# Layer 0's preparation: normalisation folded into the weights, inverse deviations as columns and a row through DRAM, three stages of blocks, merged writes

## The chip, the cores and the metric

The kernel runs on one core of one Trainium2 chip. The metric is the device time of one execution in microseconds (us), the median over several runs. The engines are TensorE (PE, with its weight loads as PEld), VectorE (DVE), ScalarE (ACT), GpSimd (POOL) and SyncE (SP), which here only issues transfers (DMA). Each engine works through its own instructions in order and waits on semaphores for the others. A DMA is issued by an engine's queue and carried out by 16 DMA engines that all queues share.

## What is computed

Two attention layers over an image `x` of 2 x 256 x 64 x 64, that is 2 batches of N = 4096 tokens with 256 channels. Only layer 0 is touched by the change; the reference for it, cut to what matters:

```python
xf = x.reshape(B, C_, N).transpose(0, 2, 1)
mu = jnp.mean(xf, axis=-1, keepdims=True)
var = jnp.mean(jnp.square(xf - mu), axis=-1, keepdims=True)
xn = (xf - mu) * jax.lax.rsqrt(var + LN_EPS) * norm_w + norm_b
qkv = jnp.einsum('bnc,oc->bno', xn, qkv_w)
q, k, v = jnp.split(qkv, 3, axis=-1)          # 4 heads of 16
attn = jax.nn.softmax(jnp.einsum('bhnd,bhmd->bhnm', q, k) * SCALE, axis=-1)
d1 = jax.nn.relu(jnp.einsum('oc,bchw->bohw', conv1_w, x) + conv1_b[None, :, None, None])
dyn = jnp.einsum('oc,bchw->bohw', conv2_w, d1) + conv2_b[None, :, None, None]
attn = attn * dyn[:, :, :, None]
out = jnp.einsum('bhnm,bhmd->bhnd', attn, v)
out = jnp.einsum('bnr,cr->bnc', out, out_w)   # back to 256 channels
return jax.nn.sigmoid(gamma[0] * out + x)
```

Layer 1 is a second attention with 4 heads of 64, without normalisation and with a residual; it takes layer 0's result.

## The kernel before

The channels lie on the partitions, in two chunks of 128 (`CC` = 2); the tokens of a batch are cut into 8 blocks of 512 (`NB`), 16 blocks in all. The kernel has three stages. The *preparation* turns each block into layer 0's q, k, v and gate. *Layer 0's attention* goes over 16 blocks of queries with 32 steps of 128 keys each (a loop over `t`), and *layer 1's attention* follows. Layer 0's attention needs the largest score of each query first (`maxima`, L398) and runs that 35 steps ahead (`LEAD0`) of the weights; the maxima of the first 32 steps therefore are taken inside the preparation, two steps in each of its last rounds.

The preparation is the loop at L603, `for n in range(len(blocks) + 3)`. Each round works on up to three blocks at different stages: `new` (block n), `middle` (n - 1) and `old` (n - 2), and the calls in the loop's body set the order on every engine, since the instructions made through `seq` keep the order of the program. Instructions made without it, DMA issues above all, are put into their queue where the scheduler finds room. For one block the steps are:

- `prep_sum` (L272, POOL): the two chunks of x are added into `both`, one block ahead of need; `prep_mean` (L279, PE): a product with a matrix of 1/256 gives the mean in every partition, in PSUM.
- `prep_center` (L284): DVE subtracts the mean (`xc`), ACT squares (`sq`), POOL adds the two chunks (`squares`).
- `prep_var`, `prep_std`, `prep_rstd` (L297 to L310), one round later: the same product for the variance, ACT's root over 128 x 512, and DVE's reciprocal in four pieces of 128 x 128.
- `prep_norm` (L312, POOL): `xc` times the inverse deviation, then times `norm_w` plus `norm_b`, a chunk at a time.
- `prep_product` (L324, PE), two rounds after the first step: q and k in one product with `wqk`. `prep_split` (L327): the result is split into three bf16 parts whose sum has the precision of fp32 (ACT, DVE, ACT, POOL), and SyncE writes them to DRAM, six pieces to `kd0` and six to `qd0` of 64 rows each, from which `load_k` (L342) and `load_q` (L390) fetch them back as 96 rows; three more rows of k are ones, set by POOL.
- `prep_values` and `prep_keep_values` (L348, L360): v by PE, copied by ACT into `vs0`. `prep_gate`, `prep_keep_gate`, `prep_dyn` (L369 to L377): conv1, its relu, and conv2 for four blocks at once.

PSUM has eight banks: four in `psw` for all products of the preparation (tag `bank`), two pairs in `psx` for the maxima. After the loop these pools are closed, the constants of the later stages are loaded, and from L751 the steps of layer 0's attention run; small jobs are hung into that loop by `at(t, place, step)`. `fold` (L414) and `turn` (L428) bring the negated maxima of a block of queries into three rows of q, and `weigh` (L440) starts with the block's first weights.

Of the kernel before, what the change touches and what calls it, by code (L numbers as in the profile page):

```python
# [32 lines left out]
def conv_attention_kernel(  # L33
# [62 lines left out]
        ]  # L96
        for s in ("sum0", "fac0")
    )
    x1 = [
        [dram.tile([C, NB], F32, tag=f"x1_{b}_{j}", name=f"x1_{b}_{j}") for j in range(NJ)]  # L100
        for b in range(B)
# [34 lines left out]
    nc.gpsimd.memset(eps, LN_EPS)  # L136

    wqk = const_prep.tile([P, CC, 2 * QK], F32, tag="wqk", name="wqk")

    spread = const0.tile([P, P], F32, tag="spread", name="spread")  # L140
    nc.gpsimd.memset(spread, 0.0)
    for h in range(H):
        nc.gpsimd.memset(spread[32 * h : 32 * h + 1, 32 * h : 32 * h + 32], 1.0)
    ident = const.tile([P, P], F32, tag="ident", name="ident")
    make_identity(nc, ident)
# [1 line left out]
    ident_b = const0.tile([P, P], BF16, tag="ident_b", name="ident_b")  # L147
    nc.gpsimd.tensor_copy(ident_b, ident)

    def fill_weights():  # L150
        nc.vector.tensor_copy(c2rep, c2.to_broadcast([P, 32]))
        for s in range(2):
            for c in range(CC):
                cols = slice(s * QK, (s + 1) * QK)
                nc.vector.tensor_copy(
                    wqk[:, c, cols].rearrange("p (d h) -> p d h", h=H),
                    qkv_raw[:, c, cols].rearrange("p (h d) -> p d h", d=D0),
                )

    def later_load(t, src):  # L160
        nc.sync.dma_start(out=t, in_=src)
# [72 lines left out]
    with own0:  # L234
        prep = own_prep.enter_context(tc.tile_pool(name="prep", bufs=2))
        own_psum = ExitStack()
        psw = own_psum.enter_context(tc.tile_pool(name="psw", bufs=4, space=PSUM))
        psx = own_psum.enter_context(tc.tile_pool(name="psx", bufs=2, space=PSUM))
        pairs = [psx]
        vs0 = [l0.tile([P, NM, P], F32, tag=f"v{b}", name=f"v_{b}") for b in range(B)]  # L240
# [1 line left out]
        def clear_v(b):  # L242

            seq(nc.gpsimd.memset(vs0[b], 0.0))
            ones_at = vs0[b].rearrange("p m (h e) -> p m h e", e=32)[:, :, :, 0:1]
            seq(nc.gpsimd.memset(ones_at, 1.0))
# [7 lines left out]
        def bank(name):  # L254
            return bank_two(name)[:, 0, :]

        def prep_bank(name):
            return psw.tile([P, NB], F32, tag="bank", name=name)

        def over_channels(ps, w, xt):  # L260
            for c in range(CC):
                seq(nc.tensor.matmul(
                    ps, w[:, c, :], xt[:, c, :], start=(c == 0), stop=(c == CC - 1)
                ))
            return ps
# [17 lines left out]

        def prep_center(b, j):  # L284
            xc = prep.tile([P, CC, NB], F32, tag="xc", bufs=3, name=f"xc_{b}_{j}")
            sq = prep.tile([P, CC, NB], F32, tag="sq", bufs=1, name=f"sq_{b}_{j}")
            mean = work.pop(("mean", b, j))
            seq(nc.vector.tensor_tensor(
                xc, xs[b, j], mean.unsqueeze(1).to_broadcast([P, CC, NB]), ALU.subtract
            ))  # L290
            seq(nc.scalar.activation(sq, xc, AF.Square))
            squares = prep.tile([P, NB], F32, tag="squares", name=f"squares_{b}_{j}")
            seq(nc.gpsimd.tensor_tensor(squares, sq[:, 0, :], sq[:, 1, :], ALU.add))
            work["xc", b, j] = xc
            work["sq", b, j] = squares

        def prep_var(b, j):  # L297
            ps = prep_bank(f"var_{b}_{j}")
            sq = work.pop(("sq", b, j))
            seq(nc.tensor.matmul(ps, mean_w, sq, start=True, stop=True))  # L300
            work["var", b, j] = ps

        def prep_std(b, j):
            std = prep.tile([P, NB], F32, tag="std", name=f"std_{b}_{j}")
            seq(nc.scalar.activation(std, work.pop(("var", b, j)), AF.Sqrt, bias=eps))
            work["std", b, j] = std

        def prep_rstd(b, j, i):
            std = work["std", b, j]
            seq(nc.vector.reciprocal(std[:, bass.ts(i, P)], std[:, bass.ts(i, P)]))  # L310

        def prep_norm(b, j):  # L312
            xc = work["xc", b, j]
            std = work.pop(("std", b, j))
            seq(nc.gpsimd.tensor_tensor(
                xc, xc, std.unsqueeze(1).to_broadcast([P, CC, NB]), ALU.mult
            ))
            for c in range(CC):
                seq(nc.gpsimd.tensor_scalar(
                    xc[:, c, :], xc[:, c, :], nw[:, c : c + 1], nb[:, c : c + 1],  # L320
                    ALU.mult, ALU.add,
                ))

        def prep_product(b, j):  # L324
            work["qk", b, j] = over_channels(prep_bank(f"qk_{b}_{j}"), wqk, work["xc", b, j])

        def prep_split(b, j):  # L327


            ps = work.pop(("qk", b, j))  # L330
            part = prep.tile([P, 3, NB], BF16, tag="part", bufs=1, name=f"part_{b}_{j}")
            rest = prep.tile([P, NB], F32, tag="rest", bufs=1, name=f"rest_{b}_{j}")
            seq(nc.scalar.copy(part[:, 0, :], ps))
            seq(nc.vector.tensor_tensor(rest, ps, part[:, 0, :], ALU.subtract))
            seq(nc.scalar.copy(part[:, 1, :], rest))
            seq(nc.gpsimd.tensor_tensor(part[:, 2, :], rest, part[:, 1, :], ALU.subtract))
            for to, of, r in ((kd0, K_PART, QK), (qd0, Q_PART, 0)):
                rows = to[b][j].rearrange("(k d) (h n) -> k (d h) n", d=D0, h=H)
                for k, i in enumerate(of):
                    nc.sync.dma_start(out=rows[k], in_=part[r : r + QK, i, :])  # L340

        def load_k(b, j):  # L342
            k = l0k.tile([P, H, NB], BF16, tag="k", name=f"k0_{b}_{j}")
            seq(nc.gpsimd.memset(k[RQ:RS], 1.0))
            nc.sync.dma_start(out=k[:RQ].rearrange("p h n -> p (h n)"), in_=kd0[b][j])
            ks0[b, j] = k

# [11 lines left out]

        def prep_keep_values(b, j):  # L360
            ps = work.pop(("v", b, j))
            seq(nc.scalar.copy(
                vs0[b][:, j * PB : (j + 1) * PB, :].rearrange(
                    "p i (h e) -> p i h e", e=32
                )[:, :, :, 1 : 1 + D0],
                ps[:, : PB * QK].rearrange("p (i h e) -> p i h e", h=H, e=D0),
            ))

        def prep_gate(b, j):  # L369
            work["d1", b, j] = over_channels(prep_bank(f"d1p_{b}_{j}"), c1, xs.pop((b, j)))  # L370
# [232 lines left out]
        for n in range(len(blocks) + 3):  # L603

            def block(k):
                return blocks[n - k] if 0 <= n - k < len(blocks) else None

            def first_maxima(i):
                x = 2 * (n - 3) + i
                if 0 <= x < NM:  # L610
                    for g in (1, 0):
                        maxima(x, g)

            new, middle, old = block(0), block(1), block(2)
            if n == 1:
                clear_v(0)
            if n == 6:
                clear_v(1)
            if new is not None:
                prep_load(*new)  # L620
                if block(-1) is not None:
                    prep_load(*block(-1))
            if n == 0:
                prep_sum(*new, nc.vector)
            if middle is not None:
                prep_var(*middle)
                prep_std(*middle)
            if new is not None:
                prep_mean(*new)
            if middle is not None:  # L630
                prep_rstd(*middle, 0)
                prep_rstd(*middle, 1)
            if new is not None:
                prep_center(*new)
            if n == 0:
                fill_weights()
            if middle is not None:
                prep_rstd(*middle, 2)
                prep_rstd(*middle, 3)
                prep_norm(*middle)  # L640
            if old is not None:
                prep_product(*old)
                prep_split(*old)
                b, j = old
                if j < (NJ, SPARE)[b]:
                    load_k(b, j)
                if old == blocks[0]:
                    load_q(old)
            if middle is not None:
                prep_gate(*middle)  # L650
                prep_keep_gate(*middle)
            first_maxima(0)
            if old is not None:
                prep_values(*old)
                prep_keep_values(*old)
            first_maxima(1)
            if middle is not None and n % 4 == 0:
                prep_dyn(blocks[n - 4 : n])
            if block(-1) is not None:
                prep_sum(*block(-1))  # L660
# [5 lines left out]
        psa = own_psum.enter_context(tc.tile_pool(name="psa", bufs=1, space=PSUM))  # L666
        pairs[0] = ps1
        gam, wo0 = more_constants()


        w1, wo1, b1, b1v, bo1, ones = layer1_constants()
# [831 lines left out]
```

## Time and profile before

| what | value |
|---|---|
| median of 3 runs | 4342.19 us (4340.53 to 4343.92) |
| the profiled execution | 4343.31 us, its span 4341.5 us |
| preparation and first maxima | from the start to about 240 us of the span |
| layer 0's attention | to about 1700 us |
| layer 1's attention | the rest |
| DMA in the first 240 us | 30.32 MB, 126 GB/s on average |

The page of the profile gives the busy time of each engine over the span, and the same in 40 slices of 108.5 us each, every digit being the busy share in tenths:

```profile
PE 4120.8 (95%) x20650; PEld 1348.3 (31%) x20650; DVE 3725.2 (86%) x3417; ACT 3422.0 (79%) x4616; POOL 2584.8 (60%) x1456
...
PE   6899999999999999899999999999999999999998
...
POOL 6600000010000000299999999999999999999995
PEclk8889999999999999999999999999999999999999
DMA  5400000010000002111112111112211112211213
```

The first two or three digits of each row are the preparation: PE at 6 and 8 tenths, POOL at 6, the granted clock of TensorE (PEclk) at 8, and DMA busier than anywhere else until the end. From the third digit PE is at 9.

In the lists below, a line such as L315 names a line of the kernel before. A group is one line, engine, operation and tile; "idle before" is the time for which the engine stood still just ahead of it, with what ended that.

### The profile page before, as it was taken

Reading aid. Unit: us, or ns where it says so; the run is one execution under the profiler, and the core shown is the slowest. Engines: PE = TensorE matmul, PEld = TensorE weight load, DVE = VectorE, ACT = ScalarE, POOL = GpSimd, SP = SyncE. Lnnn points to the kernel's source line nnn. Section 1 sums busy time; section 2 is a strip of 40 time slices with the busy share of each in tenths; the row PEclk is TensorE's granted clock in tenths of the full one; section 3 lists DMA queues with packets and bytes.
Section 4 is the critical chain, followed back from the end, with each engine's and each line's share of the span. In section 5 each row is a group of like instructions: output and inputs, shape, how many; then the busy total and the mean of one; then the engine's idle time right before and its main releaser. Section 6 shows DMA issues by size and latency. Waiting matters only on the chain. (4 is left out here: it accounts for less than half of the span.)

```text
span 4341.5 us, 56781 instructions
## 1 busy us (share of the span) xinstructions
PE 4120.8 (95%) x20650; PEld 1348.3 (31%) x20650; DVE 3725.2 (86%) x3417; ACT 3422.0 (79%) x4616; POOL 2584.8 (60%) x1456
## 2 busy tenths in 40 slices
PE   6899999999999999899999999999999999999998
PEld 3433333333333333333333333333333333222322
DVE  5778888888888883599999999999999999999997
ACT  2257777777777777698889888898898888988885
POOL 6600000010000000299999999999999999999995
PEclk8889999999999999999999999999999999999999
DMA  5400000010000002111112111112211112211213
GB/s 145 117 19 22 25 24 17 17 37 21 17 21 19 14 13 71 59 35 40 40 34 66 50 42 38 33 41 69 54 36 37 40 45 59 60 40 42 52 40 117
DMA packets 237521, 191.63 MB, mean 44 GB/s; under 512 B 155700, under 2 KB 168820, under 8 KB 237240
## 3 DMA queue, kind: packets, MB, share of 16 engines
q1 hardware_dynamic: 235384, 187.40, 16.2%
q8 instruction: 162, 2.65, 0.3%
q14 instruction: 119, 0.97, 0.1%
q10 hardware_dynamic: 1856, 0.59, 0.1%
HBM read 136.55 MB, written 51.38 MB: 43 GB/s over the span
## 5 line engine op out<-in xcount | busy, mean ns | idle before, releaser
L1027 POOL TENSOR_TENSOR acc<-acc,raw 128x1024 f32<-128x1024 f32 x821 | 1949.6, 2375 | 60.7 <-ACT raw L1015 9.3
L412 DVE TENSOR_REDUCE mx<-a 128x2 f32<-128x1024 f32 x1024 | 1209.1, 1221 | 252.5 <-PE a L407 248.2
L458 ACT ACTIVATE p<-s 128x512 f32<-128x512 f32 x1978 | 1023.4, 604 | 349.6 <-PE s L453 348.8
L931 DVE TENSOR_TENSOR rmax<-s,rmax 128x1024 f32<-128x1024 f32 x960 | 1172.7, 1222 | 139.9 <-PE s L914 128.6
L914 PE MATMUL s<-q,k 64*128 64x512 f32 x4096 | 1114.7, 636 | 105.7 <-ACT raw L932 101.3
L932 ACT COPY raw<-s 128x1024 f32<-128x1024 f32 x1024 | 1036.6, 1012 | 206.8 <-DVE rmax L931 109.8
L1003 DVE TENSOR_TENSOR raw<-raw,shift 128x1024 f32<-128x1024 f32 x961 | 1164.3, 1213 | 3.9 <-ACT shift L985 2.4
L1015 ACT ACTIVATE raw<-raw 128x1024 f32<-128x1024 f32 x1024 | 1086.6, 1062 | 78.7 <-DVE raw L1003 47.8
L1056 PE MATMUL av<-raw,v 128*64 128x512 f32 x4096 | 1008.9, 608 | 4.0 <-ACT raw L1015 2.5
L453 PE MATMUL s<-q,k 99*128 99x512 bf16 x2048 | 616.6, 381 | 15.4 <-ACT p L458 14.7
L407 PE MATMUL a<-k,q 96*128 96x512 bf16 x2048 | 612.0, 382 | 10.7 <-DVE mx L412 8.8
L471 PE MATMUL av<-p,v 128*32 128x512 f32 x4096 | 546.2, 605 | 0.2 <-ACT avs L483 0.2
L914 PEld LDWEIGHTS s<-q,k 64*128 64x128 f32 x4096 | 311.7, 185 | 707.2 <-ACT raw L932 525.6
L1056 PEld LDWEIGHTS av<-raw,v 128*64 128x64 f32 x4096 | 243.0, 136 | 651.8 <-issue 455.1
L453 PEld LDWEIGHTS <-k 99*128 99x128 bf16 x2048 | 160.8, 97 | 516.9 <-issue 390.5
L570 POOL TENSOR_SCALAR res<-res 128x1024 f32<-128x1024 f32 x16 | 16.7, 1044 | 498.1 <-ACT res L569 498.1
L407 PEld LDWEIGHTS <-q 96*128 96x128 bf16 x2048 | 200.8, 98 | 285.6 <-issue 56.5
L422 POOL CAST part<-neg 128x16 bf16<-128x16 f32 x16 | 3.4, 211 | 446.7 <-PE a L407 274.3
L519 POOL TENSOR_TENSOR f<-f,dyn 128x16 f32<-128x16 f32 x15 | 3.3, 221 | 371.8 <-DVE f L518 371.8
L1025 POOL TENSOR_TENSOR acc<-raw,raw 128x1024 f32<-128x1024 f32 x64 | 152.4, 2382 | 54.0 <-ACT raw L1015 54.0
L992 POOL TENSOR_TENSOR raw<-raw,row 128x1024 f32<-128x1024 f32 x63 | 152.2, 2417 | 39.0 <-DMA row<-neg 39.0
L471 PEld LDWEIGHTS av<-p,v 128*32 128x32 f32 x4096 | 80.9, 108 | 218.2 <-issue 210.2
(345 smaller groups left out, 2101.9 us busy)
## 6 DMA issues: line engine op xcount, KB each, us to landing
row<-neg SPq DMA_DIRECT2D x64, 512.0 KB
x<-in_x_dram SPq DMA_DIRECT2D x16, 512.0 KB
res<-in_x_dram SPq DMA_DIRECT2D x16, 512.0 KB
x<-res SPq DMA_DIRECT2D x16, 512.0 KB
att<-rows SPq DMA_DIRECT2D x62, 128.0 KB
kd<-part SPq DMA_DIRECT2D x96, 64.0 KB
qd<-part SPq DMA_DIRECT2D x96, 64.0 KB
k<-kd SPq DMA_DIRECT2D x16, 384.0 KB
```

The costliest lines, as they stand in the source:

```text
L407: seq(nc.tensor.matmul(ps[:, k, :], qs0[u][:RQ, h, bass.ts(i, P)], ks0[b, m][:RQ, h, :], start=True, stop=True,))
L412: seq(nc.vector.tensor_reduce(mxs[u][:, h : h + 2, m], ps, AX.X, ALU.max))
L453: seq(nc.tensor.matmul(ps, ks0[b, m // PB][:RS, h, bass.ts(m % PB, P)], qs0[u][:RS, h, :], start=True, stop=True,))
L458: seq(nc.scalar.activation(pt[:, k, :], ps, AF.Exp, scale=D0**-0.5))
L471: seq(nc.tensor.matmul(avs[u][32 * h : 32 * h + 32, :], vs0[b][:, m, 32 * h : 32 * h + 32], pts[t, h // 2][:, h % 2, :], start=(m == 0), s ...
L914: seq(nc.tensor.matmul(ps[:, k, :], ks[b, g, m // PB][r, bass.ts(m % PB, P)], qs1[u][r, :], start=True, stop=True,))
L931: seq(nc.vector.tensor_tensor(rmax[u, n], ps, before, ALU.max))
L932: seq(nc.scalar.copy(raw, ps))
L1003: seq(nc.vector.tensor_tensor(raws[t], raws[t], shifts[u, t % NM // GS], ALU.add))
L1015: seq(nc.scalar.activation(p, p, AF.Exp, scale=D1**-0.5))
L1027: seq(nc.gpsimd.tensor_tensor(accs[u, n], accs[u, n], p, ALU.add))
L1056: seq(nc.tensor.matmul(avs1[u, n][k * D1 : (k + 1) * D1, :], v[:, m % PB, k, :], raws[t][:, k, :], start=(m % GS == 0), stop=(m % GS == GS ...
```

## The change

- `norm_w` is multiplied into the weights once (`fill_weights`), and `norm_b` times the weights gives two columns, `bias0`, for q and k and for v. This now stands ahead of the first block's sum in round 0.
- The blocks are no longer normalised. The variance is taken as columns: four products with one column of `mean_w` give 128 x 4 values, one for each token; ACT's root and DVE's reciprocal work on 128 x 4. v is scaled by these columns when ACT copies it out of PSUM, in four pieces. For q and k, which have tokens along the free dimension, the columns are written to DRAM (`rst0`, element by element) and read back as one row into all 128 partitions (`rrow`); DVE multiplies the product with it, and the bias for q and k is added in the split.
- The bias for v is added later: with weights that add up to one it is a constant for each channel of a head, and goes into `wo0`, in three small steps hung into the first steps of the attention loop.
- The rounds are set anew: product, values and gate are all of the `middle` block, the scaling and the split of the `old` one. The product has a PSUM bank of its own (tag `qk`), the other products share three.
- Writes to `kd0` and `qd0` are merged: each of the three parts goes out once, repeated in the source where it is wanted more than once, six writes instead of twelve. The rows of ones of k come by DMA from a small array in DRAM that is filled once from ACT's queue.
- x is loaded two blocks ahead instead of one.

```diff
+    rst0 = [
+        [dram.tile([1, NB], F32, tag=f"rst0_{b}_{j}", name=f"rst0_{b}_{j}") for j in range(NJ)]
+        for b in range(B)
+    ]
+    ones0 = dram.tile([RS - RQ, H * NB], BF16, tag="ones0", name="ones0")
...
+    for h in range(H):
+        nc.scalar.dma_start(out=ones0[:, bass.ts(h, NB)], in_=one_rows)
...
-    def fill_weights():
+    def fill_weights(ps):
...
+        for i, w in enumerate((wqk, wv_pad)):
+            for c in range(CC):
+                nc.tensor.matmul(
+                    ps[:, i : i + 1], w[:, c, :], nb[:, c : c + 1],
+                    start=(c == 0), stop=(c == CC - 1),
+                )
+        nc.vector.tensor_copy(bias0, ps[:, :2])
+        for w in (wqk, wv):
+            for c in range(CC):
+                nc.vector.tensor_scalar(w[:, c, :], w[:, c, :], nw[:, c : c + 1], None, ALU.mult)
...
         def prep_var(b, j):
             ps = prep_bank(f"var_{b}_{j}")
             sq = work.pop(("sq", b, j))
-            seq(nc.tensor.matmul(ps, mean_w, sq, start=True, stop=True))
...
+            for i in range(PB):
+                seq(nc.tensor.matmul(
+                    ps[:, i : i + 1], sq[:, bass.ts(i, P)], mean_w[:, :1], start=True, stop=True
+                ))
+            std = prep.tile([P, PB], F32, tag="std", name=f"std_{b}_{j}")
+            seq(nc.scalar.activation(std, ps[:, :PB], AF.Sqrt, bias=eps))
+            work["rcol", b, j] = std
+
+        def prep_rstd(b, j):
+            std = work["rcol", b, j]
+            seq(nc.vector.reciprocal(std, std))
+            with nc.allow_non_contiguous_dma(reason="a column to a row"):
+                nc.sync.dma_start(
+                    out=rst0[b][j].rearrange("o (i p) -> p (o i)", p=P), in_=std
+                )
+            row = prep.tile([P, NB], F32, tag="rrow", bufs=1, name=f"rrow_{b}_{j}")
+            nc.sync.dma_start(out=row, in_=rst0[b][j].partition_broadcast(P))
+            work["rrow", b, j] = row
...
+        def prep_scale(b, j):
+            rest = prep.tile([P, NB], F32, tag="rest", name=f"rest_{b}_{j}")
+            part = prep.tile([P, 3, NB], BF16, tag="part", bufs=1, name=f"part_{b}_{j}")
+            row = work.pop(("rrow", b, j))
+            seq(nc.vector.tensor_tensor(rest, work.pop(("qk", b, j)), row, ALU.mult))
+            seq(nc.scalar.activation(part[:, 0, :], rest, AF.Identity, bias=bias0[:, :1]))
+            work["part", b, j] = part, rest
+
+        def prep_split(b, j):
+            part, rest = work.pop(("part", b, j))
+            seq(nc.vector.scalar_tensor_tensor(
+                rest, rest, bias0[:, :1], part[:, 0, :], ALU.add, ALU.subtract
             ))
-            for c in range(CC):
-                seq(nc.gpsimd.tensor_scalar(
-                    xc[:, c, :], xc[:, c, :], nw[:, c : c + 1], nb[:, c : c + 1],
-                    ALU.mult, ALU.add,
-                ))
...
             for to, of, r in ((kd0, K_PART, QK), (qd0, Q_PART, 0)):
-                rows = to[b][j].rearrange("(k d) (h n) -> k (d h) n", d=D0, h=H)
-                for k, i in enumerate(of):
-                    nc.sync.dma_start(out=rows[k], in_=part[r : r + QK, i, :])
+                rows = to[b][j].rearrange("(k d) (h n) -> (d h) k n", d=D0, h=H)
+                for i in range(3):
+                    k = [k for k, of_k in enumerate(of) if of_k == i]
+                    step = k[1] - k[0] if len(k) > 1 else 1
+                    nc.sync.dma_start(
+                        out=rows[:, k[0] : k[-1] + 1 : step, :],
+                        in_=part[r : r + QK, i : i + 1, :].to_broadcast([QK, len(k), NB]),
+                    )

         def load_k(b, j):
             k = l0k.tile([P, H, NB], BF16, tag="k", name=f"k0_{b}_{j}")
-            seq(nc.gpsimd.memset(k[RQ:RS], 1.0))
+            nc.sync.dma_start(out=k[RQ:RS].rearrange("p h n -> p (h n)"), in_=ones0)
...
+            rcol = work.pop(("rcol", b, j))
+            for i in range(PB):
+                seq(nc.scalar.activation(
+                    vs0[b][:, j * PB + i, :].rearrange("p (h e) -> p h e", e=32)[
+                        :, :, 1 : 1 + D0
+                    ],
+                    ps[:, bass.ts(i, QK)].rearrange("p (h e) -> p h e", e=D0),
+                    AF.Copy, scale=rcol[:, i : i + 1],
+                ))
...
+            for k in (0, -1, -2) if n == 0 else (-2,):
+                if block(k) is not None:
+                    prep_load(*block(k))
+            if n == 0:
+                fill_weights(prep_bank("bias"))
+                prep_sum(*new, nc.vector)
+            if old is not None:
+                prep_scale(*old)
+            if new is not None:
+                prep_mean(*new)
+                prep_center(*new)
             if middle is not None:
                 prep_var(*middle)
-                prep_std(*middle)
...
+                prep_rstd(*middle)
+            if new is not None:
+                prep_squares(*new)
             if old is not None:
-                prep_product(*old)
                 prep_split(*old)
...
             if middle is not None:
+                prep_product(*middle)
+            first_maxima(0)
+            if middle is not None:
+                prep_values(*middle)
+                prep_keep_values(*middle)
                 prep_gate(*middle)
                 prep_keep_gate(*middle)
-            first_maxima(0)
-            if old is not None:
-                prep_values(*old)
-                prep_keep_values(*old)
             first_maxima(1)
...
+        def value_bias(step):
+            if step == 0:
+                seq(nc.gpsimd.tensor_scalar(sel, sel, bias0[:, 1:2], None, ALU.mult))
+            elif step == 1:
+                work["wo"] = bank("wo_bias")
+                seq(nc.tensor.matmul(work["wo"][:, :C], sel, wo0, start=True, stop=True))
+            else:
+                seq(nc.vector.tensor_tensor(wo0, wo0, work.pop("wo")[:, :C], ALU.add))
+
+        for step in range(3):
+            at(-LEAD0 + NM + step, ("start", "end", "start")[step], lambda step=step: value_bias(step))
```

In the changed program's order of instructions, SyncE has for each round, one after the other: the column out to `rst0`, the first two writes of `kd0`, the row back from `rst0`, the last write of `kd0`, the three of `qd0`, the load of k and a load of x. DVE has the product with the row, the centring, the reciprocal, the split, then four maxima. PE has mean, variance, the product for q and k, two pairs of maxima, the values, the gate, and the other two pairs.

## The prediction

> **What bounds the kernel now.** I read the busy time by stretches first, then the list of waits, then the timelines of GpSimd and of SyncE's queue. The stretches (busy us of PE, PEld, DVE, ACT, POOL, then granted clock, DMA share, GB/s):
>
> ```profile
> 50.00:100.00 50.00, 38.45 (x131) 18.02 (x130) 35.96 (x37) 13.98 (x21) 35.84 (x27) 0.90 0.49 135
> 150.00:200.00 50.00, 40.04 (x147) 20.43 (x147) 35.63 (x36) 15.09 (x23) 32.91 (x26) 0.86 0.48 128
> 200.00:250.00 50.00, 41.48 (x154) 18.67 (x153) 38.83 (x39) 13.83 (x22) 15.58 (x17) 0.76 0.29 72
> 500.00:600.00 100.00, 98.89 (x560) 30.64 (x556) 81.52 (x72) 72.84 (x139) 3.41 (x7) 1.00 0.11 34
> ```
>
> From about 250 us on PE is 99% busy at full clock. Before it, in the preparation, no engine is full: PE and DVE are at 71 to 83%, POOL at 66 to 72% until 200 us, which is the picture of a loop through several engines. The waits of the first 420 us (us in total, times, longest) name the loop:
>
> ```profile
> ACT sq L291 <- DVE xc L288: 72.2, 15, 7.9
> POOL squares L293 <- ACT sq L291: 65.9, 16, 7.5
> PE mean L281 <- POOL both L276: 40.5, 13, 5.2
> DVE xc L288 <- PE mean L281: 28.8, 10, 4.8
> ```
>
> `both` (POOL), mean (PE), `xc` (DVE), `sq` (ACT), `squares` (POOL): a ring, closed by POOL's own order, as its timeline for one block shows (start, length, idle before):
>
> ```profile
> 43.58 1.27 POOL L293 TENSOR_TENSOR squares<-sq 128x512 f32<-128x512 f32 x1 [4.62 <-ACT sq L291]
> 44.80 2.35 POOL L315 TENSOR_TENSOR xc<-xc,std 128x1024 f32<-128x1024 f32 x1
> 47.26 1.52 POOL L319 TENSOR_SCALAR xc<-xc,nw,nb 128x512 f32<-128x512 f32 x2
> 48.74 1.16 POOL L336 TENSOR_TENSOR part<-rest,part 128x512 bf16<-128x512 f32 x1
> 49.95 1.80 POOL L344 MEMSET k<- 3x2048 bf16 x1
> 51.83 1.26 POOL L276 TENSOR_TENSOR both<-x 128x512 f32<-128x512 f32 x1
> 56.76 1.26 POOL L293 TENSOR_TENSOR squares<-sq 128x512 f32<-128x512 f32 x1 [3.67 <-ACT sq L291]
> ```
>
> POOL works 9.4 us and then waits 3.7 to 4.6 for mean, centring and squaring of the next block. The centrings (L288) of blocks 4 and 15 start at 54.31 and 204.48: 150.17 us for 11 blocks, 13.65 each, somewhat over this block's 13.18, since after POOL's long turns the mean runs at half clock (2.08 instead of 1.12 us, at 135.63).
>
> **The change, part by part.**
>
> *POOL.* Normalisation (2.35 + 1.52) and the memset (1.80) go: 5.67 us a block. What is left is 1.26 + 1.15 + 1.26 = 3.7, far from binding.
>
> *DVE.* Four reciprocals of 128x128 (0.88 each) become one of 128x4, at about the 0.24 of L518's 128x16. Added: the product with the row (0.69, as L334); L334 itself becomes the three-operand form (0.75, as L560). A block: 0.69 + 1.16 + 0.24 + 0.75 + 4 maxima at 1.16 = 7.5 us.
>
> *ACT.* The root of 128x512 (0.69) becomes 128x4, about 0.25; one copy of 128x256 (0.39) becomes four of 128x64, about 0.24 each by the slope between 128x256 (0.39) and 128x512 (0.58). A block stays at some 4.3 us: covered.
>
> *PE.* Unchanged but the variance: four products of one column. The values' 16 records take 1.73, so 8 records 0.9, as before. A block at full clock, by distances between starts: mean 0.95, variance 0.9, qk 1.72, values 1.73, gate 1.72, maxima 2 x 0.87 = 8.8, and 1.9 for dyn every fourth block.
>
> *The new ring.* qk has one bank: qk of a block waits until DVE's product with the row has read the one before. Counted from that product's end (0): qk starts at 0.1, ends 1.8; two maxima pairs 2.7; values 4.4; gate 6.15; the other two 6.6 and 7.0. DVE meanwhile: centring to 1.2, reciprocal 1.45, split 2.2, two maxima by 4.9, idle until 6.6 + 0.25 (the hop from a product to its reduction), then two maxima (2.36 together) to 9.2, and the next product to 9.9. Period 9.9. Every fourth block dyn stands ahead of mean and variance, and qk starts some 0.75 later: 0.2 on average, 10.1.
>
> *The trip through DRAM.* Reciprocal, 2 KB column out, row of 256 KB back, product. No such pair is in this stage; layer 1 has one, `neg` out (256 pieces of 8 bytes) and `row` back (512 KB), in SyncE's queue, with the share of DMA while `neg` is written, and the first row with its reader:
>
> ```profile
> 1878.40 3.23 SPq L964 DMA_DIRECT2D neg<-negs  x2
> 1884.42 0.33 SPq L969 DMA_DIRECT2D row<-neg  x1
> ```
>
> ```profile
> 1882.00:1882.50 0.50, 0.50 (x6) 0.09 (x2) 0.44 (x1) 0.50 (x1) 0.43 (x1) 1.00 0.29 4
> ```
>
> ```profile
> 1809.60 0.34 SPq L969 DMA_DIRECT2D row<-neg  x1
> 1813.38 1.09 ACT L985 COPY shift<-row 128x1024 f32<-128x1024 f32 x1 [0.71 <-DMA row<-neg]
> ```
>
> The second `neg` is issued at 1881.27 and releases `row` at 1884.42: 3.15 us. The row is used 3.78 after its issue; half the bytes save about 1.15 of transfer: 2.6. The trip is 5.8: started at 1.5 it ends at 7.3, wanted at 9.2, so 1.9 us are free. SyncE puts two kd writes between the two halves; the second waits for ACT's copy (about 2.9) and is issued by 3.6, before the column has landed (4.65): no delay. Behind the row stand the last kd write, three of qd, the load of k and the next x: at 0.62, 0.53 and 0.40 they end near 9, before the next column at 11.6. The bounds: 0 late, if the rings are empty; if the k and x loads (896 KB, 2.8 us at the 320 GB/s that 41 to 45 us show) are all ahead of it, 0.9 late. I take 0.3: period 10.4. `part` has one buffer: ACT's first write waits until qd has been read, up to 1 us late, within DVE's idle 1.9.
>
> The Trainium skill speaks against this step ("DMA: Bandwidth & Descriptors", Rules for kernel authors): a transfer whose last dimension is not contiguous becomes one descriptor for each element, and it gives 19 times for a transpose made so. The row at 1882 shows 0.29 of 0.5 us, 0.15 us of all engines, for 256 such pieces; 512 would be 0.3. By the rule's factor, an estimate, 0.15 would be 2.8 us, the trip 8.4, the period 8.4 + 2.15 + 0.3 = 10.85 and the gain 40 instead of 44.
>
> *Merged writes.* Twelve issues of about 0.63 us become six. Bytes are the same; with the row, a block moves 1.9 MB in 10.4 us, 185 GB/s against 128 now. No cost beyond the lateness above. The ones of k by DMA are issued at the start, behind four small writes on ACT's queue: 2.4 us of SyncE while it has nothing due.
>
> *The start.* The weights are now finished ahead of the first sum: it began at 4.89; it must now wait for the raw weights (6.96), six copies (1.0), the bias products (about 1.5 on a cold PE), five small DVE operations (1.2): about 10.5. So block 0 is centred 5.4 us later. Without POOL's turns the next blocks follow faster, even with a trip each: the variance of block 0 follows the mean of block 1 (to 20.8), its reciprocal ends at 21.5, and a trip (with 0.7 of issue and hops) brings the first product with a row at 28; centring 2 ends at 29.4, the next trip at 36; the last qd of block 0 is issued by 35.5, is written near 38, and its q lands near 40.5, where PE waits for it; qk, pairs, values and gate after that put the fourth maximum and block 3's product before 48.6, and block 4's centring at 49.0 against 54.31. Gain 5.3.
>
> *The body.* 11 x (13.65 - 10.4) = 35.8.
>
> *The end.* From the last centring to the first fold (L421, 239.49) it took 35.0. Now: one more period (9.9), qk to the fourth maximum and product 9.9, split 1.45, eight maxima 9.3: 30.6. Gain 4.4.
>
> *Value bias.* Three small steps hung in the next stage, where PE is full: POOL's are free, the PE product of 256 columns is 0.43 and borrows a bank of the maxima: bounds 0 and 2, I take 1.0.
>
> Sum: 5.3 + 35.8 + 4.4 - 1.0 = 44.5 off the profiled execution's 4343.31 (span 4341.5 and 1.8 around it): 4298.8. The median shown is 1.1 lower: 4297.7, so 4298. What follows keeps its length, since PE bounds it and starts it with the fold.
>
> **The rivals.**
>
> *A: the trip becomes the ring.* Product, centring, reciprocal (2.15) and the trip follow each other: the period is the trip plus 2.15, once the trip exceeds 8. For it: SyncE issues in order, and one landing not yet there holds all behind it. Against: 5.8 measured. With a trip of 10 the period is 12.2: 5.3 + 16 + 4.4 - 1 = 25 off, 4317.
>
> *B: slower.* The same trip with all its company: if its tiny pieces, the 1 KB pieces of kd and the loads go through the rings one behind the other, and the trip passes 13.1, the period passes 15.2, where 11 x 1.55 and another 0.2% eat the 8.7 gained at the ends. At 14: period 16.2, 11 x 2.55 - 8.7 = 19 more, 4361. For it: DMA is busy at 0.9 to 1.26 at 43 to 45 us. Against: only for some 3 us a block.
>
> *C: nothing comes through,* because the next stage starts by something else: 4342. Against: its first product (247.32) follows ACT's copy of q, POOL's parts, the fold at 239.49 and the maxima, with gaps of about 1 us.
>
> *D: a shorter ring.* If dyn and lateness cost nothing and the start loses less, 9.8: 5.3 + 42 + 4.4 - 0 + 3 = 55, 4287.
>
> **How the numbers follow.** Forecast 0.62, A 0.25, B 0.05, C 0.03, D 0.05. The range reaches from D, 4287, to A, 4318. 0.2% is 8.7 us, about what tells a difference from none here: faster 0.92 (forecast, A, D), same 0.03, slower 0.05.
>
> **What would show it.** Centrings 10 to 10.8 us apart; POOL idle two thirds of the preparation; DVE idle before the third maximum of a block, waiting for PE; the granted clock near 1.0; the product with the row starting right behind the fourth maximum, not behind a DMA. If DVE waits there for the row, A holds; if the first fold is near 190 us and the end isn't 44 earlier, the value bias or the later loads of layer 1's weights have taken it back.

## The result, and the profile after

| | before | after |
|---|---|---|
| time, median (us) | 4341.36 (4 runs, 4338.76 to 4343.92) | 4411.26 (4 runs, 4410.29 to 4418.58) |
| span of the profiled execution | 4341.5 | 4408.5 |
| centring of block 4, of block 15 | 54.31, 204.48 | 73.66, 261.34 |
| us per block between them | 13.65 | 17.06 |
| first fold | 239.49 | 305.51 |

The changed kernel takes 1.0165 times as long, 95% interval [1.0147, 1.0182]. It was forecast at 4298, faster. The forecast's own four terms, set beside the trace of after:

| term | forecast | measured | too low by |
|---|---|---|---|
| centring of block 4 | 49.0 | 73.66 | 24.7 |
| eleven blocks | 11 x 10.4 = 114.4 | 187.68 | 73.3 |
| last centring to first fold | 30.6 | 44.17 | 13.6 |
| what comes after the fold | 1.0 | 67.0 (spans) - 66.0 (folds) = 1.0 | 0 |

That is 111.6; 4298.8 + 111.6 = 4410.4, and the profiled execution took 4408.5 + 1.8 around it = 4410.3. The four terms make up the whole span, so their sum has to come out; what the table shows is that the miss lies ahead of the first fold and that nothing is to be looked for behind it. The preparation's waits in the first 350 us, in total, times and longest:

```profile
POOL squares L326 <- ACT sq L324: 200.1, 16, 15.8
DVE rest L361 <- DMA rrow<-rst: 97.1, 15, 14.8
PE qk L292 <- DVE rest L361: 89.1, 15, 7.5
ACT part L362 <- DMA qd<-part: 88.9, 11, 10.2
```

and in SyncE's own queue:

```profile
SPq L350 <- DMA rst<-std: 136.1, 16, 9.7
```

POOL's long wait now costs nothing: its turn was cut as forecast, and it idles. The row (`rrow`) is late for DVE's product (L361) in 15 of 16 blocks, PE stands behind that product with its one `qk` bank, and in the queue a row waits 8.5 us (136.1 / 16) for its column (`rst`) to land. *Landing* means here the time from a transfer's issue until the next instruction that waits for it goes on; the *trip* is the landing of the column and the row together, up to DVE's product. The timeline of the first trip, with nothing but small transfers beside it:

```profile
21.67 0.39 SPq L346 DMA_DIRECT2D rst<-std  x1
32.23 0.35 SPq L350 DMA_DIRECT2D rrow<-rst  x1
36.16 0.69 DVE L361 TENSOR_TENSOR rest<-qk,rrow 128x512 f32<-128x512 f32 x1 [14.53 <-DMA rrow<-rst]
```

From the column's issue to the row's, 10.56 us. What the DMA engines did meanwhile (stretch, its length, busy time of PE, PEld, DVE, ACT, POOL, then granted clock, DMA share, GB/s):

```profile
22.50:23.00 0.50, 0.50 (x2) 0.17 (x1) 0.00 (x0) 0.00 (x0) 0.50 (x1) 1.00 0.51 4
23.00:23.50 0.50, 0.50 (x2) 0.17 (x1) 0.00 (x0) 0.00 (x0) 0.50 (x1) 1.00 0.13 33
24.00:32.00 8.00, 6.22 (x31) 4.18 (x30) 0.00 (x0) 1.62 (x5) 0.93 (x1) 1.00 0.00 1
```

In the first of these half microseconds they were busy for 0.51 x 0.5 = 0.26 us; from 24 to 32 us they showed nothing, and only then was the write reported as done. A block later on:

```profile
74.99 0.38 SPq L346 DMA_DIRECT2D rst<-std  x1
84.30 0.35 SPq L350 DMA_DIRECT2D rrow<-rst  x1
89.22 0.69 DVE L361 TENSOR_TENSOR rest<-qk,rrow 128x512 f32<-128x512 f32 x1 [6.24 <-DMA rrow<-rst]
89.83 1.21 DVE L317 TENSOR_TENSOR xc<-x,mean 128x1024 f32<-128x1024 f32 x1
89.97 2.93 PE L292 MATMUL qk<-xc,wqk 128*128 128x512 f32 x3 [6.12 <-DVE rest L361]
```

Column 9.3, row 4.9, a trip of 14.2 us, and 2.5 more to the next column (91.71): 16.7. Over blocks 4 to 14 the trip is 14.5 on average and the way from the product to the next column 2.6. The last line shows a second cost: after a wait of 6.1 us PE goes on at half speed (2.93 for three products that take 1.55 at full clock, at 73.80). The granted clock of 100 to 200 us is 0.80, against 0.86 before.

### The profile page after: what moved, and what is told of

It reads as the page before. It is cut to its first block, busy times and chain, and to the rows that moved or that the text cites. A ratio compares the mean times of both kernels' runs of the same rounds, so it can differ in the third digit from the quotient of the medians.

```text
span 4408.5 us, 56938 instructions
## 1 busy us (share of the span) xinstructions
PE 4130.8 (94%) x20756; PEld 1366.0 (31%) x20756; DVE 3684.2 (84%) x3393; ACT 3425.2 (78%) x4664; POOL 2497.9 (57%) x1400
## 5 line engine op out<-in xcount | busy, mean ns | idle before, releaser
L452 PE MATMUL a<-k,q 96*128 96x512 bf16 x2048 | 614.5, 383 | 16.2 <-DVE mx L457 8.6
```

Of the source, the lines that this page charges most:

```text
L452: seq(nc.tensor.matmul(ps[:, k, :], qs0[u][:RQ, h, bass.ts(i, P)], ks0[b, m][:RQ, h, :], start=True, stop=True,))
```

## The experiments

The question was why the column takes 10 us to land. Three theories: its pieces are too small, they are too many, or the queue and its company (the transfers that run beside it) hold them up. All four kernels below are the changed kernel with the trip altered.

**Pairs of 8 bytes** (256 pieces; the row lies in DRAM in that order, and the product reads it by pairs):

```
-    out=rst0[b][j].rearrange("o (i p) -> p (o i)", p=P), in_=std
+    out=rst0[b][j].rearrange("o (a p i) -> p (o a) i", p=P, i=2),
+    in_=std.rearrange("p (a i) -> p a i", i=2),
```

> The column is written as 256 pieces of 8 bytes (pairs, as layer 1 does), the row's order follows and the product reads it with a stride of two; nothing else changes. Theory S (the size of a piece decides: 4-byte pieces land late): SyncE waits about 3.2 us for the column instead of 9 to 10, the trip is 8, the centrings stand about 10.4 apart, 4300 us. Rival N (the number of pieces decides, some 7 us for 512): half of it, a landing near 6, period 13, about 4355. Rival Q (the company in the queue and the rings decides): as the changed kernel, 4411.

**Half the row** (256 pieces of 4 bytes, `std[:, :PB // 2]`, read twice by the product):

> 256 pieces of 4 bytes: only the deviations of a block's first 256 tokens go to DRAM, and the row of 256 is used for both halves of the block (so the other half of q and k is scaled with the wrong tokens' deviations). Theory S, if each 4-byte piece costs the same: landing near 6, period 13, 4355; if a fixed cost of 4-byte writes: 9 to 10 as in the changed kernel, about 4400. Rival N: near 6 too.

**512 pieces of 8 bytes** (each value written twice, `std.unsqueeze(2).to_broadcast([P, PB, 2])` copied to a tile; the row has twice the bytes, and `xc` two buffers instead of three):

> 512 pieces of 8 bytes: each deviation is written twice side by side, the row is 4 KB a partition and the product takes every second value. Theory S: landing 3.2 to 3.5, a row of 512 KB 1.2 us later than one of 256, period about 11 to 11.5, 4310. Rival N: landing 9 to 10 as in the changed kernel, about 4420.

**No trip** (POOL spreads the column over 512 columns, PE turns it with four products by the identity, ACT copies the row out of PSUM; `xc` has two buffers instead of three):

```
+    rep = prep.tile([P, PB, P], F32, tag="rep", bufs=1, name=f"rep_{b}_{j}")
+    seq(nc.gpsimd.tensor_copy(rep, std.unsqueeze(2).to_broadcast([P, PB, P])))
+ def prep_row(b, j):
...
+    for i in range(PB):
+        seq(nc.tensor.matmul(ps[:, bass.ts(i, P)], rep[:, i, :], ident, start=True, stop=True))
+    seq(nc.scalar.copy(row, ps))
```

> No trip at all: POOL spreads the column over 128x512, PE turns it into the row by four products with the identity behind the fourth maximum, ACT copies it out of PSUM. Theory T (the trip alone made the changed kernel slow, and the rest of the working holds): DVE is the ring, period 10.1 to 10.6, first fold near 190 us of the span, 4295 to 4305. Rival R (something else of the change costs too, the one buffer of parts, the half clock of PE or the new order of the rounds): period 13 or more, 4345 or more.

Measured (landing is from the column's issue to the row's; "first" is the first block, "later" the range and mean of blocks 3 to 15):

| kernel | column | landing first; later | us per block | first fold | time (us) | ratio to before |
|---|---|---|---|---|---|---|
| after | 512 x 4 B | 10.6; 9.3 to 11.7, 10.5 | 17.06 | 305.51 | 4411.26 | 1.0165 [1.0147, 1.0182] |
| half the row | 256 x 4 B | 8.8; 9.2 to 11.7, 10.3 | 16.9 | 300.25 | 4407.39 | one run |
| twice the row | 512 x 8 B | 4.7; 3.9 to 6.6, 5.3 | 12.70 | 236.45 | 4346.54 | one run |
| pairs | 256 x 8 B | 4.5; 3.7 to 6.9, 5.6 | 12.31 | 232.09 | 4337.05 | 0.9989 [0.9979, 0.9998] |
| no trip | none | none | 10.09 | 198.00 | 4303.96 | 0.9914 [0.9898, 0.9931] |

The number of pieces falls as a cause: 512 of 8 bytes land sooner than 256 of 4. The queue falls as the main one: the same transfers stand ahead and behind in all rows with a trip. In later blocks the 8-byte columns land 0.6 to 1.1 us later on average than the first one does; which of the transfers beside them does that was not tested. Theory S had the right order of the kernels and was too early with its times (4337 for 4300 with pairs, 4347 for 4310 with twice the row), since the trip still sets the period:

```profile
98.45 0.36 SPq L346 DMA_DIRECT2D rst<-std  x1
104.07 0.34 SPq L351 DMA_DIRECT2D rrow<-rst  x1
107.80 0.69 DVE L363 TENSOR_TENSOR rest<-qk,rrow 128x512 f32<-128x512 f32 x1 [2.08 <-DMA rrow<-rst]
```

(the kernel with pairs: landing 5.6, row 3.7, a trip of 9.35, and DVE still waits 2.08 for it; it does in 12 of 16 blocks.) The kernel without the trip shows the rest of the change doing what was forecast. DVE's timeline there:

```profile
96.68 1.21 DVE L313 TENSOR_TENSOR xc<-x,mean 128x1024 f32<-128x1024 f32 x1
97.81 0.17 DVE L340 RECIPROCAL std<-std 128x4 f32<-128x4 f32 x1
97.90 0.72 DVE L372 SCALAR_TENSOR_TENSOR rest<-rest,bias,part 128x512 f32<-128x512 f32 x1
99.28 2.36 DVE L460 TENSOR_REDUCE mx<-a 128x2 f32<-128x1024 f32 x2 [0.66 <-PE a L455]
103.65 2.36 DVE L460 TENSOR_REDUCE mx<-a 128x2 f32<-128x1024 f32 x2 [2.01 <-PE a L455]
105.92 0.68 DVE L364 TENSOR_TENSOR rest<-qk,rrow 128x512 f32<-128x512 f32 x1
```

It waits for PE ahead of the third maximum (2.01 us) and for nothing ahead of the product, as the forecast's last part asked; 10.09 us a block, and the granted clock of 100 to 170 us is 1.00.

**The probe.** So far "4 bytes are slow" and "8 bytes are fast" fit. The probe measures the disputed write by itself:

```
t = dram.tile([1, size], dt, tag=tag, name=tag)
seq(nc.sync.dma_start(out=view(t), in_=src))          # the form
seq(nc.sync.dma_start(out=back[:, :1], in_=t[:, :1])) # waits for it
```

> The kernel leaves the whole computation out: it writes zeros to the output and then, three times over, writes twelve small forms to DRAM from SyncE, each followed by a read of one element that waits for it. The landing of a form is the time from its issue to the issue of its read; the first turn runs beside the output's writes, the second and third alone. Theory S (the size of a piece decides): 512, 256, 128 and 16 pieces of 4 bytes all land 8.5 to 10.5 us after issue, 512 and 256 pieces of 8 bytes in 4.4 to 5, 128 of 16 bytes and 4 of 512 bytes in 2.5 to 4.5, 512 pieces of 2 bytes no sooner than 8.5. Rival N (the number of pieces): landings fall with the number, 16 pieces of 4 bytes under 4, 512 of 8 bytes near 10. Rival L (neighbours in one small stretch of memory, written by different engines, get in each other's way): 4-byte pieces that stand 64 or 512 bytes apart land like 8-byte pieces, under 5 us, and those 16 bytes apart lie between.

SyncE's queue in the third turn, five of the forms, each with the read that waits for it (the last pair is the form with 64 bytes between pieces):

```profile
163.26 0.38 SPq L72 DMA_DIRECT2D n512x4B<-col  x1
173.58 0.22 SPq L75 DMA_DIRECT2D back_n512x4B<-n512x4B  x1
...
194.57 0.39 SPq L72 DMA_DIRECT2D n512x8B<-col  x1
199.20 0.23 SPq L75 DMA_DIRECT2D back_n512x8B<-n512x8B  x1
...
204.07 0.35 SPq L72 DMA_DIRECT2D n128x16B<-col  x1
205.49 0.22 SPq L75 DMA_DIRECT2D back_n128x16B<-n128x16B  x1
205.75 0.25 SPq L72 DMA_DIRECT2D n4x512B<-four  x1
207.92 0.21 SPq L75 DMA_DIRECT2D back_n4x512B<-n4x512B  x1
...
211.34 0.38 SPq L72 DMA_DIRECT2D n512x4B_by<-col  x1
213.13 0.22 SPq L75 DMA_DIRECT2D back_n512x4B_by<-n512x4B_by  x1
```

All forms, second and third turn, by how many pieces fall into 64 bytes of DRAM:

| form | pieces in 64 bytes | landing (us) |
|---|---|---|
| 512 x 2 B, side by side | 32 | 15.3, 14.5 |
| 512, 256, 128 x 4 B, side by side | 16 | 9.3, 10.3; 9.1, 9.3; 7.8, 7.8 |
| 16 x 4 B, side by side | 16, in one stretch | 2.4, 2.5 |
| 512, 256 x 8 B, side by side | 8 | 3.3, 4.6; 3.2, 4.3 |
| 512 x 4 B, 16 bytes apart | 4 | 2.7, 2.9 |
| 128 x 16 B, side by side | 4 | 2.6, 1.4 |
| 512 x 4 B, 64 and 512 bytes apart | 1 | 2.3, 1.8; 1.8, 1.8 |
| 4 x 512 B | under 1 | 1.2, 2.2 |

My theory of the size falls here, and the rival that I gave least thought holds: the same 512 pieces of 4 bytes land in 1.8 us when they lie 64 bytes apart and in 10 when they lie side by side. What counts is how many pieces share a short stretch of memory. How long that stretch is the probe doesn't settle. Counted in 64 bytes, the 16 pieces of 4 bytes are an exception (2.4, though their stretch is full). Counted in 512 bytes, all forms fall into order: 256 pieces 14.5 to 15.3, 128 pieces 7.8 to 10.3, 64 pieces 3.2 to 4.6, 32 pieces 1.4 to 2.9, 16 pieces 2.4, 8 pieces 1.8 to 2.3, one piece 1.2 to 2.2. Beyond that the number of pieces matters little (4-byte pieces: 128 in 7.8, 256 in 9.2, 512 in 9.3 to 10.3).

**16 bytes a piece** is the change that this calls for: a partition's four values side by side.

```
-    out=rst0[b][j].rearrange("o (i p) -> p (o i)", p=P), in_=std
+    out=rst0[b][j].rearrange("o (p i) -> p (o i)", p=P), in_=std
...
+    row.rearrange("p (m i) -> p i m", i=PB), ALU.mult,
```

> The change as it is, but the column goes out as 128 pieces of 16 bytes (a partition's four values side by side), the row lies in DRAM in that order, and the product with the row reads it 16 bytes apart. The probe had adjacent pieces of 16 bytes landing in 1.4 to 2.6 us, of 8 bytes in 3.2 to 4.6, of 4 bytes in 9.1 to 10.3, and 4-byte pieces that lie 16 bytes apart in 2.7 to 2.9, 64 apart in 1.8 to 2.3. Theory L (pieces that share a short stretch of memory get in each other's way) with theory T (the ring is trip plus about 2.9): the landing in company falls from 5.6 (8 bytes) to 3 to 3.5, the trip to about 7, which no longer binds; the period is that of PE and DVE, 10.1 to 10.5, and the time 4300 to 4310, I say 4305. Rival Q (queue and company hold the column up whatever its pieces): it stays near that of the 8-byte pieces, 12.3 a block, 4330 to 4337. If DVE pays for the stride, the product with the row is longer than 0.69.

Measured 4310.74 (4307.44 to 4314.35), ratio 0.9930 [0.9915, 0.9945]; 10.55 us a block. One block near 93 us:

```profile
93.24 0.32 SPq L346 DMA_DIRECT2D rst<-std  x1
95.35 0.48 SPq L350 DMA_DIRECT2D rrow<-rst  x1
98.73 2.36 DVE L462 TENSOR_REDUCE mx<-a 128x2 f32<-128x1024 f32 x2 [2.01 <-PE a L457]
101.00 1.04 DVE L362 TENSOR_TENSOR rest<-qk,rrow 128x512 f32<-128x512 f32 x1
```

The column lands in 2.1 (4.1 in the next block, at 103.29; 3.3 on average over blocks 3 to 15), and the product follows the maxima with no wait for the row. It does wait in 4 of 16 blocks: 6.0 and 7.0 in the first two, 0.5 and 1.4 in two later ones. The first trip takes 2.5 + 3.5 = 6.0, where the forecast had 5.8. The order of four values in memory moves the change from 1.6% slower to 0.7% faster; DVE pays 1.04 instead of 0.69 for reading the row 16 bytes apart.

**Turned by PE, 4 pieces of 512 bytes** (a transpose behind the `qk` product, an ACT copy, then the write).

> The column is turned by a PE transpose into four rows, ACT copies them and they go to DRAM as 4 pieces of 512 bytes; the row is read back as before. xc has two buffers to make room. Theory S: the landing drops from 9.3 in company to 3 to 4.5 us, the row takes 3.7, and the ring (product 0.7, centring and reciprocal to 1.45, transpose behind the first half of qk and copy to 2.6, landing, row) is 10 to 11.5 us a block: 4304 to 4320, I say 4313. Rival Q (anything written out and read back through SyncE's queue in company is this late): the landing stays over 8, the period near 17, 4400. Theory T says that whatever the trip measures plus about 2.9 is the period.

Measured 4364.63 in one run, 14.45 us a block, worse than 4313 and better than 4400: neither theory's number.

```profile
107.71 0.69 DVE L364 TENSOR_TENSOR rest<-qk,rrow 128x512 f32<-128x512 f32 x1 [3.47 <-DMA rrow<-rst]
...
109.45 0.17 DVE L344 RECIPROCAL std<-std 128x4 f32<-128x4 f32 x1
112.03 0.42 PE L348 MATMUL turned<-ident,std 128*4 128x128 f32 x1
112.49 0.26 ACT L350 COPY four<-turned 4x128 f32<-4x128 f32 x1 [1.36 <-PE turned L348]
...
115.01 0.43 SPq L351 DMA_DIRECT2D rst<-four  x1
117.92 0.41 SPq L353 DMA_DIRECT2D rrow<-rst  x1
123.67 0.69 DVE L364 TENSOR_TENSOR rest<-qk,rrow 128x512 f32<-128x512 f32 x1 [3.44 <-DMA rrow<-rst]
```

The write lands in 2.9 here and in 1.5 to 5.6 over the blocks, 2.2 on average over blocks 3 to 15 (1.2 and 2.2 in the probe), so the short landing that theory S asked for came out. But the column is issued 5.6 us after the reciprocal: 2.6 until the transpose starts behind the `qk` product on PE, and 2.3 from the end of ACT's copy until SyncE has issued the writes of kd and qd ahead of it; and the row takes 5.75. From product to column it is 7.3 instead of 2.6, from column to product 8.7, and their sum is this block's 16.0 (107.71 to 123.67).

**Merged writes undone** in the kernel without the trip: `for k, i in enumerate(of): nc.sync.dma_start(out=rows[k], in_=part[r : r + QK, i, :])`.

> The kernel whose row is made by PE, with the twelve single writes of kd and qd of the kernel before in place of six merged ones. Merged, six writes hold SyncE's queue for about 6.3 us a block (4.38 + 1.89); twelve at 0.63 hold it for 7.5, and with the loads of k and x 8.4 of 10.1. If writes are hidden by the ring through PE and DVE: 10.1 to 10.3 a block, 4302 to 4307. Rival: the one buffer of part is read out later, ACT's first write into it waits, and the ring is up to 1.2 longer: 4317.

Measured 4333.30 (4331.14 to 4335.92), ratio 0.9980 [0.9971, 0.9989]; 11.31 us a block, fold 23.3 later than with merged writes. The rival holds, and its price for a block too (1.22 for 1.2); its time, 4317, left out the start (block 4 is centred 2.9 later) and the end (7.0 longer):

```profile
99.32 3.78 SPq L380 DMA_DIRECT2D qd<-part  x6
103.21 0.53 SPq L385 DMA_DIRECT2D k<-kd  x1
103.83 0.40 SPq L109 DMA_DIRECT2D x<-in_x_dram  x1
105.71 4.90 SPq L380 DMA_DIRECT2D kd<-part  x6
```

Twelve issues hold SyncE 8.7 us, the last qd is issued near 103, and ACT's write into the one buffer of `part` waits for its landing:

```profile
ACT part L365 <- DMA qd<-part: 50.1, 10, 7.5
```

(waits of the first 250 us; merged, the same wait is 2.3 in total.) Merging is worth 29 us of this kernel, of which 23.3 lie in the preparation; the rest came after the fold in that trace, where other traces differ by up to 6 us too, and was not followed.

**The first q ahead of a load of x**, and **an early start** (block 0 centred before the weights are finished, POOL's sum of block 1 before the squares of block 0), both in the kernel without the trip; then the early start with 16-byte pieces.

> The kernel whose row is made by PE, with the load of x of block 5 (512 KB) behind the first loads of k and q in SyncE's queue instead of ahead of them. If the first q is late because 1.3 MB (x, k, q) share 6.5 us of the rings: k and q alone are 786 KB, q lands near 42.5 instead of 45.1, PE waits some 2 instead of 4.6 us and keeps its clock, block 4 is centred near 51.5 instead of 56.4, and the time is 4299 to 4301. If q is late by its own writes: it lands after 44.5, nothing moves, 4302 to 4306.

> The kernel whose row is made by PE, with block 0 summed and centred before the weights are finished, and block 1 summed by POOL before the squares of block 0. The first centring moves from 12.5 to about 9.3, the second from 19.5 to about 12.5. If the start is a chain of work, block 4's centring moves up by 5 to 7 us from 56.4, and the time is 4297 to 4300. If the rings (the loads of x, k and q) or the half clock of PE set it, less than 2 of that is left: 4302 to 4305.

> Both: 16-byte pieces and the early start. If the two are independent, as much under the kernel with 16-byte pieces as the early start brings by itself: 4296 to 4304. The rival is that the first trips stand in the start's chain and take the gain back: the same as with 16-byte pieces alone, within 2.

| kernel | first q: issued, used | block 4 centred | time (us) | ratio to before |
|---|---|---|---|---|
| no trip | 39.94, 45.19 | 56.39 | 4303.96 | 0.9914 [0.9898, 0.9931] |
| q ahead of x | 42.03, 47.41 | 60.01 | 4308.27 | 0.9917 [0.9900, 0.9933] |
| early start | 32.04, 37.67 | 48.87 | 4296.48 | 0.9898 [0.9881, 0.9914] |
| 16-byte pieces | 41.24, 46.63 | 59.47 | 4310.74 | 0.9930 [0.9915, 0.9945] |
| both | 35.58, 40.71 | 53.55 | 4304.93 | 0.9921 [0.9906, 0.9936] |

Putting x behind q did not make q land sooner: in all five kernels it takes 5.1 to 5.6 us from its issue, with the DMA engines mostly at 0.7 to 1.2 meanwhile. That doesn't clear the load of x, which was only moved from 1.4 us ahead of q to 0.4 us behind it and shares the DMA engines with it in both orders; what q would take without it isn't shown. The edit also moved the start (block 2 is centred at 33.05 instead of 30.50, q issued 2.1 later), and the time missed both of its forecasts. The start is a chain of work: begun 4 us earlier, block 4 comes 7.5 earlier and the first fold too (190.47 for 198.00). 4296.48 is the best time of all, below both given kernels; its interval overlaps that of the kernel without the trip, but all four of its runs (4294.78 to 4297.97) lie below all four of the other (4302.05 to 4307.02). With 16-byte pieces the early start gains 5.8 in the medians, but the two intervals overlap and the two traced spans are alike (4312.6 and 4312.9), so that gain isn't shown.

## Why the prediction was wrong

- **The step that failed: the trip through DRAM.** The forecast put the trip at 5.8 us, with 1.9 to spare, and so kept it out of the ring. It took the column's landing, 3.15, from `neg` (256 pieces of 8 bytes; 2.9 to 5.1 over its 64 uses in the trace of before) and checked only what the DMA engines would be busy for: "0.15 us of all engines, for 256 such pieces; 512 would be 0.3". Both figures were right in themselves (the engines took 0.26), and neither is the landing. The column's 512 pieces of 4 bytes side by side land in 9.3 to 11.7. The row was sized too low as well: 3.3 to 4.9, 3.9 on average, for 2.6. No run shows the 1.15 that half the bytes were to save: where DVE waited for it, a row of 512 KB (twice the row) took 4.5 on average, of 256 KB 3.9, of 128 KB (half the row) 3.9. The trip is 14.5 for 5.8.
- **The rule of rival A** (the period is the trip plus 2.15) was the right mechanism, at a trip longer than the 10 it was priced at: 14.5 + 2.6 here, 9.9 + 2.5 with pairs (means of blocks 4 to 14), and with 16-byte pieces a trip that binds in few blocks. The 2.6 in place of 2.15 has a reason in the trace: ACT's first write into `part` waits for the landing of qd, which the forecast had put "within DVE's idle 1.9", and the root and the reciprocal stand behind it. In one block the product starts at 105.50, that write at 107.69, the reciprocal at 108.59, and the next column goes out 3.3 after the product.
- **Rival B**, at 0.05, named this outcome, a trip of 14, and its period there, 16.2, is near the 17.06 measured; but not its cause. It blamed the company in the rings, and the first column, with only small transfers beside it, took 10.56 as well. Its time, 4361, is 50 too low, since it kept the 8.7 gained at the ends. A trip stands in the start and in the end as well: block 4 came 19.4 later than before and the end was 9.2 longer. The body cost 11 x 3.41 = 37.5, and 37.5 + 19.4 + 9.2 + 1.0 is the 67 us lost. The bounds for the landing (0 and 0.9 late) covered company alone as well, not a form of write that the trace of before did not hold.
- **Clock.** The forecast of a granted clock near 1.0 hung on a short ring. It holds without the trip (1.00 over 100 to 170 us); with the long one PE waits some 6 us a block, runs on at half speed, and the clock is 0.80.
- **Right, shown by the kernel without the trip:** 10.09 a block (10.1 forecast), last centring to fold 30.57 (30.6), DVE's wait ahead of the third maximum, POOL no longer binding. What comes after the fold cost 1.0 as forecast in after; in the other traces the span and the fold have moved by amounts 0.3 to 6.2 us apart, so the value bias by itself is not measured, and the agreement is partly luck.
- **Merged writes** were given no worth beyond their queue time; in the kernel without the trip they carry 29 us: with twelve, the release of `part` becomes the ring's next wait.
- **The start** was 7.4 too early even without the trip (56.39 for 49.0), and 10.5 with 16-byte pieces, whose first trip is as long as forecast: q was to land 2.5 us after its write, and takes 5.2 from its issue, in which PE waits 4.6, and then runs at half clock for the next 7 us.
- **The Trainium skill's rule** ("DMA: Bandwidth & Descriptors", Rules for kernel authors: a last dimension that is not contiguous becomes one descriptor for each element) pointed at the right line. The estimate made from it, a trip of 8.4, fell 6 short of the 14.5, and its factor multiplied a time that was already that of single pieces. The runs do not show the number of elements as the cause: the probe's 4-byte pieces 64 bytes apart are just as many single elements and land in 1.8 to 2.3.

With 16-byte pieces the same terms read: 10.55 a block for 10.4, the end 33.0 for 30.6, block 4 at 59.5 for 49.0. That puts 1.7 + 2.4 + 10.5 on 4298.8: 4313.4, against 4314.4 for its profiled execution. So with a short trip the period was nearly right, and what is left of the miss is the start.

## What to carry to other kernels

A transfer's time on the DMA engines says nothing of when it lands; where a wait hangs on a landing, take the landing of the same form (size of a piece and how the pieces lie in memory), or write the form in a probe before it is built on. A column written to DRAM element by element should go with each partition's elements side by side, or with its pieces apart, and the reader should take up the order. And a term that is put into the period belongs in the start and in the end too.

## What the runs showed of the hardware

- Small writes to DRAM land the later the more of them share a short stretch, counted here in 512 bytes: 256 pieces 14.5 to 15.3 us, 128 pieces 7.8 to 10.3, 64 pieces 3.2 to 4.6, 32 or fewer 1.2 to 2.9, while the engines were busy with the 4-byte column for 0.26 us. Why, and how long the stretch is, was not settled. The Trainium skill ("DMA: Bandwidth & Descriptors", Specifications) says that a transfer below 512 bytes is done as read-modify-write; pieces that must wait for one another in a shared stretch would fit that. But 4-byte pieces 64 bytes apart land in 1.8 to 2.3, about as soon as the 512-byte ones (1.2 and 2.2), so smallness by itself costs no time that shows here, and no run shows the mechanism.
- In the first turn of the probe the first write, queued behind 8 MB of output, took 29 us to land (10.43 to 39.40), against 9.3 and 10.3 for the same write alone: a landing contains what stands ahead of it.
- After a PE wait of 3.4 to 6 us PE ran on at half speed: for some 4 us behind the waits for the row in after (5.6 and 6.1 us; granted clock 0.50 until 93.5 and 110.5), for 7 to 10 us behind the wait for the first q (3.4 to 4.8 us; 16 products of the values 3.51 instead of 1.9 us). What sets that length was not followed.
